# 72 directly summed columns in three bf16 addends, with the codes copied by GpSimd

## The chip, the cores and the metric

The kernel runs on one core of one Trainium2 chip. That core has a matrix engine (PE, with its weight loads shown as PEld), a vector engine (DVE), an activation engine (ACT), a general engine (POOL, also called GpSimd) and a sequencer that only issues transfers (SP). Each works through a queue of its own, in order; they meet at semaphores. The metric is the device time of the kernel in microseconds. Before the change it is 2163.95 us, the median of three runs from 2160.82 to 2169.29.

## The reference

A graph layer over 6250 nodes with 128 features. There are 206250 edges, each with a row of 128 floats and a node number `src` that stands in no order. The edge rows are summed per node, and a small network follows with a residual and a layer norm:

```python
row = edge_index[0]                                   # src, 206250 numbers in 0..6249
edge_aggr = jnp.zeros((n, 128)).at[row].add(edge_attr)
combined = concatenate([x, edge_aggr, global_feat repeated], -1) @ W_c + b_c
h = softplus(combined @ W1 + b1)
h = softplus(h @ W2 + b2)
out = layernorm(x + h @ W3 + b3)
```

Nearly all of the time goes into `edge_aggr`, the scatter-add.

## The kernel before, in words

An edge *column* is 128 edges, one on each partition; there are 1611 full ones and a rest of 42 edges. Nodes are cut into 25 *blocks* of 256. `sums_t` holds the sums of all nodes on chip, features on the partitions and nodes along the free axis.

**The sorted way.** Most columns are cut into ten groups (`GROUPS`). For a group, `positions` works out on DVE and PE at which row of a buffer in HBM (`place`) each edge has to stand, so that edges of one block lie together. POOL then issues one indirect DMA per column (`scatter_rows`, L644), which writes 128 rows of 129 floats: the 128 features and a *code*, the node's number within its block plus an offset that belongs to the group. The rows come from HBM in pieces of ten columns (`load_rows`, three pieces ahead, five buffers), and the code of each edge is copied into the row's last float by `code_rows`, on ACT, two pieces ahead (L636). When a group is in place, `reduce_steps` reads it back in chunks on SP, DVE compares the codes with a row of numbers to make a 0/1 matrix `hot` (L423), PE multiplies rows by it (L437) and DVE adds the result to the block's part of `sums_t` (L454). For the last two groups ACT makes three of four `hot` matrices (L418, L420), since DVE has more to do there. While group g is scattered, group g-1 is summed and the positions of group g+1 are made. Three `place` buffers go round, and are filled with -1 at first.

**The direct way.** The first 48 columns (`DIRECT`) are not scattered. For each column and each window of 512 nodes, ACT makes a 0/1 matrix out of |node - number| (L577, two columns) and relu(1 - that) (L579, both at once), PE multiplies the edge rows by it (L589, f32), and after 12 columns (`SET`) DVE adds the window's sum to `sums_t` (L593). A *job* is two columns (`QUAD`) by one window; PE's part of a job stands two jobs behind ACT's. `begin` prepares `less`, the node numbers less each window's first node, for all columns at once.

**The order of the work.** PE, DVE, ACT and SP run in an order written out by hand: for every piece of every group, the row load, the code copy and the scatters are emitted, then a share of the steps for positions, sums, node rows, fills and direct jobs. The shares go by `AHEAD`, and the direct steps go to groups 1 to 6 in proportion to `left`, an estimate of the column times that a group has to spare. All of SP's transfers stand in one queue, so a chunk load that waits for a buffer holds up the row loads behind it. POOL alone is ordered by the scheduler. The network at the end starts when all sums are there.

The code that tells which share goes where:

```python
left[g] = max(0.0, groups[g][1] - groups[g][0]
              - groups[g - 1][3] * groups[g - 1][2] / 3 - (9 if 3 <= g < 6 else 0))
```

Of the kernel before, what the change touches and what calls it, by code (L numbers as in the profile page):

```python
# [7 lines left out]
F32 = mybir.dt.float32  # L8
BF16 = mybir.dt.bfloat16
# [7 lines left out]
P = 128  # L17
# [2 lines left out]
LOAD_COLS = 10  # L20
EPS = 1e-5

GROUPS = ((40, 1), (120, 2), (200, 4), (240, 4), (240, 4), (240, 4), (212, 4), (140, 2), (88, 2),
          (44, 1))
CHUNK_ROWS = 1024
PLACES = 3

DIRECT = 48
SET = 12
WIDE = 512  # L30
QUAD = 2
FILL = 4
POS_COLS = 20
PART_COLS = 60
# [6 lines left out]
LEAD = 3  # L41
# [6 lines left out]
def kernel(  # L48
# [119 lines left out]
    with ExitStack() as phase:  # L168
# [376 lines left out]
        def direct_steps():  # L545


            steps = []
            if not ND:
                return steps  # L550
            NW = -(-NB * BL // WIDE)
            less = keep.tile([P, NW, ND], F32, name="less")
            rows_in, hot_of, sum_of = {}, {}, {}

            def begin():

                first = keep.tile([P, NW], F32, name="first")
                nc.gpsimd.iota(first, pattern=[[WIDE, NW]], base=0, channel_multiplier=0,
                               allow_small_or_imprecise_dtypes=True)
                part, node, _ = whole_nodes(0, ND)  # L560
                nc.vector.tensor_copy(node, part)
                nc.vector.tensor_tensor(
                    less, node.unsqueeze(1).to_broadcast([P, NW, ND]),
                    first.unsqueeze(2).to_broadcast([P, NW, ND]), op=ALU.subtract)

            def load(c):
                n = min(SET, ND - c)
                rows_in[c] = direct_p.tile([P, SET, D], F32, name="direct_rows", bufs=2)
                sync_dma(rows_in[c][:, :n],
                         edge_attr[:P * T, :].rearrange("(p t) d -> p t d", p=P)[:, c:c + n, :])  # L570

            def compare(c, w, q):
                n = min(WIDE, NB * BL - w * WIDE)
                hot = direct_p.tile([P, QUAD, WIDE], F32, name="direct_hot", bufs=4)
                hot_of[c, w, q] = hot
                for j in range(QUAD):
                    nc.scalar.activation(hot[:, j, :n], iota_f[:, :n], AF.Abs,  # L577
                                         bias=less[:, w, c + q + j:c + q + j + 1], scale=-1.0)
                nc.scalar.activation(hot[:, :, :n], hot[:, :, :n], AF.Relu, bias=ones[:, :1],  # L579
                                     scale=-1.0)  # L580

            def add(c, w, q):
                n = min(WIDE, NB * BL - w * WIDE)
                k = min(SET, ND - c)
                hot = hot_of.pop((c, w, q))
                if q == 0:
                    sum_of[c, w] = ps.tile([P, WIDE], F32, name="direct_sum", bufs=2)
                for j in range(QUAD):
                    nc.tensor.matmul(sum_of[c, w][:, :n], rows_in[c][:, q + j, :], hot[:, j, :n],  # L589
                                     start=(q + j == 0), stop=(q + j == k - 1))  # L590
                if q + QUAD == k:
                    here = sums_t[:, w * WIDE:w * WIDE + n]
                    nc.vector.tensor_add(here, here, sum_of.pop((c, w))[:, :n])  # L593

            jobs = [(c, w, q) for c in range(0, ND, SET) for w in range(NW)
                    for q in range(0, min(SET, ND - c), QUAD)]
            steps += [begin, lambda: load(0)]
            for i in range(len(jobs) + 2):
                def one(i=i):
                    if i < len(jobs):  # L600
                        c, w, q = jobs[i]
                        if (w, q) == (NW // 2, 0) and c + SET < ND:
                            load(c + SET)
                        compare(*jobs[i])
                    if i > 1:
                        add(*jobs[i - 2])
                steps.append(one)
            return steps
# [22 lines left out]

        def code_rows(i):
            if i >= len(pieces):
                return
            g, c, k, r = pieces[i]
            nc.scalar.copy(rows_at[i][:r, :k, D:W], low[:r, c:c + k].unsqueeze(2))  # L636

        def scatter_rows(i):
            g, c, k, r = pieces[i]
# [12 lines left out]
        with tc.manual_schedule(engines={ET.PE, ET.DVE, ET.Activation, ET.SP}):  # L652
# [20 lines left out]
            while put["todo"]:  # L673
                put["todo"].pop(0)()
            node_codes(ND, c1)
            for i in range(LEAD - 1):
                code_rows(i)
            for step in positions(0):
                step()
            sync_dma(wc_sb, w_c.rearrange("(k p) d -> p k d", p=P))  # L680
# [10 lines left out]
            for g in range(1, G - 3):  # L691
                left[g] = max(0.0, groups[g][1] - groups[g][0]
                              - groups[g - 1][3] * groups[g - 1][2] / 3 - (9 if 3 <= g < 6 else 0))
            direct_at = 0.0
            i = 0
            assert G > 6
            nodes = []
            for g in range(G):
# [11 lines left out]
                filled = fill_rows(g + 1)  # L710
                done = [0, 0, 0, 0]
                for q in mine:
                    load_rows(i + LEAD)
                    code_rows(i + LEAD - 1)
                    scatter_rows(i)
                    i += 1

                    now = []
                    for w, todo in enumerate((prep, sums, other, filled)):
                        share = (q - mine[0] + 1) / len(mine)  # L720
                        if w == 2:
# [175 lines left out]
```

## Time and profile before

| what | value |
|---|---|
| median of three runs | 2163.95 us |
| the profiled execution's own time | 2166.67 us |
| its span, first to last instruction | 2164.9 us |
| mean granted clock of PE | 0.925 |
| scatters on POOL (L644) | 1564, 961 ns each, first at 25.57 us, last at 2018.42 us |
| direct products on PE (L589) | 1248 instructions, 559.0 us busy |
| sorted products on PE (L437) | 4472 instructions, 1106.0 us busy |
| direct matrices on ACT (L577, L579) | 624 and 312, 404.6 and 348.0 us busy |
| code copies on ACT (L636) | 159, 30.7 us busy |

A line of the list of groups reads: line of the kernel, engine, operation, what it writes and reads, count, then the busy time and the mean of one, then the idle time of that engine just before these instructions and what ended most of it. A line of a timeline reads: start, length, engine, line, operation, count, and in brackets the idle time before it with its releaser. A line of windows gives, for a stretch of the span, its length, the busy time and count of PE, PEld, DVE, ACT and POOL, then the granted clock, the share of the DMA engines and GB/s. A line of waits gives who waited for whom, the total, how often and the longest. "issue" means that the engine waited for nothing that the profile shows. Busy times of PE contain the length of a product through its pipeline, so products that follow each other closely overlap: their pitch, from start to start, is what they cost.

The groups' scatters start at 25.6, 81.2, 233.1, 486.2, 789.9, 1102.6, 1406.2, 1675.6, 1852.7 and 1964.0 us.

### The profile page before, as it was taken

How to read it: one execution, taken by the hardware profiler on the slowest of the kernel's cores; microseconds unless marked ns; L12 is line 12 of the kernel's file. 1: busy time of each engine (PE TensorE's matmuls, PEld its weight loads, DVE VectorE, ACT ScalarE, POOL GpSimd, SP SyncE). 2: the span in 40 equal slices, each digit the busy share in tenths (PEclk: the TensorE clock that was granted, in tenths of full speed). 3: DMA queues.
4: the chain of work that ended last, by engine and by line, in shares of the span. 5: the costliest groups of instructions: out<-in, count | busy, mean ns of one | idle time of the engine just before them, and what ended most of it. 6: DMA issues, size and time to landing. Idle time of an engine off the chain costs nothing.

```text
span 2164.9 us, 22230 instructions
## 1 busy us (share of the span) xinstructions
PE 1789.7 (83%) x6415; PEld 1209.0 (56%) x6415; DVE 1328.0 (61%) x1923; ACT 912.7 (42%) x1350; POOL 1560.2 (72%) x1631
## 2 busy tenths in 40 slices
PE   3398788966889878999889998788998899688884
PEld 0144445534555555666556666556666778566752
DVE  7386457524656345675465855355755798796567
ACT  0476665653444335444353443353342000006964
POOL 5777777777777767777777777777777777777226
PEclk8699999987999999999999999999999999899997
DMA  9998788738786665676756666556766687776521
GB/s 299 303 313 270 216 256 251 231 101 262 213 225 189 194 193 148 188 207 188 198 173 180 194 190 175 169 167 189 202 198 170 211 245 227 214 213 199 151 75 60
DMA packets 415376, 435.50 MB, mean 201 GB/s; under 512 B 37743, under 2 KB 305766, under 8 KB 415254
## 3 DMA queue, kind: packets, MB, share of 16 engines
q1 hardware_dynamic: 365062, 330.71, 54.9%
q0 software_dynamic: 50048, 103.35, 14.4%
q8 instruction: 51, 0.84, 0.2%
q14 instruction: 71, 0.58, 0.1%
q10 hardware_dynamic: 144, 0.02, 0.0%
HBM read 260.90 MB, written 173.03 MB: 200 GB/s over the span
## 4 chain that ended last, share of the span: by engine, by line
PE 57%; DVE 15%; POOL 9%; issue 7%; DMA 6%; ACT 4%; DVEq 1%; SPq 0%; POOLq 0%; ACTq 0%
PE part L437 37%; PE direct_sum L589 16%; POOL place L644 8%; DVE hot L423 7%; DMA place<-rows,pos 4%; DVE sums_t L454 2%; ACT hot L418 2%; DVE so_far L316 1%; DVE sums_t L593 1%; DMA rows<-in_edge_attr 1%; DMA chunks<-place 1%; PE small L339 1%; POOL y L833 1%; DVEq L448 1%; DVE pos L350 1%
## 5 line engine op out<-in xcount | busy, mean ns | idle before, releaser
L644 POOL DMA_INDIRECT place<-rows,pos x1564 | 1503.2, 961 | 509.0 <-issue 443.5
L437 PE MATMUL part<-hot,chunks 128*128 128x256 f32 x4472 | 1106.0, 405 | 267.8 <-DVE hot L423 250.9
L437 PEld LDWEIGHTS part<-hot,chunks 128*128 128x128 f32 x4472 | 894.9, 203 | 507.8 <-DVE hot L423 310.5
L577 ACT ACTIVATE direct_hot<-iota_f,less 128x512 f32<-128x512 f32 (+1 forms) x624 | 404.6, 695 | 811.0 <-PE direct_sum L589 808.1
L423 DVE SCALAR_TENSOR_TENSOR hot<-chunks,iota_ps 128x2048 f32<-128x2048 f32 (+1 forms) x261 | 592.2, 2270 | 44.2 <-DMA chunks<-place 44.2
L589 PE MATMUL direct_sum<-direct_hot,direct_rows 128*128 128x512 f32 (+1 forms) x1248 | 559.0, 580 | 29.4 <-DMA direct_rows<-in_edge_attr 25.6
L454 DVE TENSOR_TENSOR sums_t<-sums_t,part 128x256 f32 x781 | 327.1, 419 | 133.3 <-PE part L437 110.8
L589 PEld LDWEIGHTS direct_sum<-direct_hot,direct_rows 128*128 128x128 f32 x1248 | 233.3, 190 | 232.2 <-issue 204.9
L579 ACT ACTIVATE direct_hot<-direct_hot,ones 128x1024 f32<-128x1024 f32 (+1 forms) x312 | 348.0, 1115 | 10.1
L593 DVE TENSOR_TENSOR sums_t<-sums_t,direct_sum 128x512 f32<-128x512 f32 (+1 forms) x52 | 34.7, 667 | 410.5 <-PE direct_sum L589 410.5
L636 ACT COPY rows<-src_i 128x10 f32<-128x10 f32 (+1 forms) x159 | 30.7, 196 | 360.3 <-DMA place<-rows,pos 328.9
L350 DVE TENSOR_REDUCE pos<-at 128x20 int32<-128x500 f32 (+2 forms) x80 | 87.0, 1087 | 2.7
L316 DVE TENSOR_TENSOR_SCAN so_far<-iota_ps,ib 128x1500 bf16<-128x1500 f32 (+5 forms) x29 | 85.7, 2955 | 0.0
L418 ACT ACTIVATE hot<-iota_f,chunks 128x256 f32<-128x256 f32 x156 | 64.2, 493 | 26.7 <-DMA chunks<-place 24.2
L845 POOL TENSOR_TENSOR x_sb<-x_sb,b_all 128x512 f32<-128x512 f32 (+1 forms) x13 | 15.2, 1219 | 67.8 <-DMA x_sb<-in_x 67.8
L348 DVE TENSOR_TENSOR at<-small,ib 128x500 f32<-128x500 f32 (+2 forms) x80 | 52.9, 661 | 4.2 <-PE small L339 3.5
L833 POOL TENSOR_SCALAR y<-y,mv,rs 128x128 f32<-128x128 f32 (+1 forms) x45 | 35.2, 796 | 19.9 <-DVE rs L827 19.0
L262 DVE TENSOR_TENSOR ib<-block,iota_ps 128x1500 bf16<-128x1500 bf16 (+5 forms) x29 | 44.2, 1550 | 0.0
L273 PE MATMUL small<-ib,ones_h 128*128 128x500 bf16 (+2 forms) x80 | 23.8, 406 | 23.9 <-DVE ib L262 23.9
L536 DVE TENSOR_SCALAR z_x<-small,z_bias 128x512 f32<-128x512 f32 (+1 forms) x13 | 9.3, 718 | 51.3 <-PE small L534 51.3
L335 PE MATMUL small<-so_far,ones_h 128*128 128x500 bf16 (+2 forms) x80 | 31.4, 393 | 11.1 <-DVE last L319 11.1
L420 ACT ACTIVATE hot<-hot,ones 128x2048 f32<-128x2048 f32 (+1 forms) x20 | 39.2, 1960 | 0.7
(115 smaller groups left out, 472.7 us busy)
## 6 DMA issues: line engine op xcount, KB each, us to landing
chunks<-place SPq DMA_DIRECT2D x278, 516.0 KB, 4.5
rows<-in_edge_attr SPq DMA_DIRECT2D x155, 640.0 KB, 6.7
place<-fill SPq DMA_DIRECT2D x252, 258.0 KB, 8.3
place<-rows,pos POOLq DMA_INDIRECT x1564, 4.5
x_sb<-in_x SPq DMA_DIRECT2D x24, 256.0 KB, 4.6
direct_rows<-in_edge_attr SPq DMA_DIRECT2D x4, 768.0 KB
out<-y SPq DMA_DIRECT2D x12, 256.0 KB, 2.2
chunks<-place SPq DMA_DIRECT2D x3, 258.0 KB, 3.2
```

The lines of the kernel that those rows point to most:

```text
L316: nc.vector.tensor_tensor_scan(t, iota_ps[:, 1:2].to_broadcast([P, NB * n]), in_block[k][0], 0.0, op0=ALU.mult, op1=ALU.add)
L350: nc.vector.tensor_reduce(pos[:, a - c0 + j0:a - c0 + j1], at.rearrange("p b g -> p g b"), axis=mybir.AxisListType.X, op=ALU.add)
L418: nc.scalar.activation(hot[:, j], codes, AF.Abs, bias=chunks[i][:, j, D:W], scale=-1.0)
L423: nc.vector.scalar_tensor_tensor(hot[:, :m], chunks[i][:, :m, D:W].to_broadcast([P, m, BL]), code_of(g), iota_ps.unsqueeze(1).to_broadcast ...
L437: nc.tensor.matmul(part[:, s - q, :], t[:, s * sub + j, :D], hot[:, s * sub + j], start=(j == 0), stop=(j == sub - 1))
L454: nc.vector.tensor_add(here, here, part[:, s - q, :])
L577: nc.scalar.activation(hot[:, j, :n], iota_f[:, :n], AF.Abs, bias=less[:, w, c + q + j:c + q + j + 1], scale=-1.0)
L579: nc.scalar.activation(hot[:, :, :n], hot[:, :, :n], AF.Relu, bias=ones[:, :1], scale=-1.0)
L589: nc.tensor.matmul(sum_of[c, w][:, :n], rows_in[c][:, q + j, :], hot[:, j, :n], start=(q + j == 0), stop=(q + j == k - 1))
L593: nc.vector.tensor_add(here, here, sum_of.pop((c, w))[:, :n])
L644: s = nc.gpsimd.indirect_dma_start(out=dst, out_offset=bass.IndirectOffsetOnAxis(ap=at, axis=0), in_=rows[:r, j, :], in_offset=None)
L833: engine.tensor_scalar(y[:r, q, :], y[:r, q, :], mv[:r, at + q, 0:1], rs[:r, 1, at + q:at + q + 1], op0=ALU.subtract, op1=ALU.mult)
```

## The change

- `DIRECT` is 72 instead of 48, and the seventh group (group 6, counted from 0) has 188 columns instead of 212. The other groups keep their sizes and take their columns 24 further on.
- The direct products are made in bf16. An f32 row is split into three bf16 numbers that add up to it: its upper 16 bits (read in place), the upper 16 bits of the rest, and what remains. The second is written over the lower 16 bits of the row, the third into `direct_low`. `split` does this on DVE for 12 columns at a time, two columns per instruction (`SPLIT`). PE reads the first two with a stride of two and makes three bf16 products where one f32 product stood. The 0/1 matrix is made in bf16.
- `less` is made per set of 12 columns in `split` instead of once in `begin`.
- The first direct load is issued before the last piece of group 0, ahead of that piece's row load; it was in group 1.
- `code_rows` runs on POOL in front of the piece's own scatters, instead of on ACT two pieces ahead.

```diff
-GROUPS = ((40, 1), (120, 2), (200, 4), (240, 4), (240, 4), (240, 4), (212, 4), (140, 2), (88, 2),
+GROUPS = ((40, 1), (120, 2), (200, 4), (240, 4), (240, 4), (240, 4), (188, 4), (140, 2), (88, 2),
           (44, 1))
-DIRECT = 48
+DIRECT = 72
+SPLIT = 2
...
-            less = keep.tile([P, NW, ND], F32, name="less")
+            node_f = keep.tile([P, ND], F32, name="node_f")
+            first = keep.tile([P, NW], F32, name="first")
...
-                part, node, _ = whole_nodes(0, ND)
-                nc.vector.tensor_copy(node, part)
-                nc.vector.tensor_tensor(
-                    less, node.unsqueeze(1).to_broadcast([P, NW, ND]),
-                    first.unsqueeze(2).to_broadcast([P, NW, ND]), op=ALU.subtract)
+                part, _, _ = whole_nodes(0, ND)
+                nc.vector.tensor_copy(node_f, part)
...
+            def halves(t):
+                return [t.bitcast(BF16).rearrange("p c (d h) -> p c d h", h=2)[:, :, :, h]
+                        for h in (0, 1)]
+
+            def split(c):
+                n = min(SET, ND - c)
+                less = less_of[c] = direct_p.tile([P, NW, SET], F32, name="less", bufs=2)
+                nc.vector.tensor_tensor(
+                    less[:, :, :n], node_f[:, c:c + n].unsqueeze(1).to_broadcast([P, NW, n]),
+                    first.unsqueeze(2).to_broadcast([P, NW, n]), op=ALU.subtract)
+                low_in[c] = direct_p.tile([P, SET, D], BF16, name="direct_low", bufs=2)
+                for a in range(0, min(SET, ND - c), SPLIT):
+                    b = min(a + SPLIT, SET, ND - c)
+                    rest = direct_p.tile([P, SPLIT, D], F32, name="direct_rest")[:, :b - a]
+                    x_c = rows_in[c][:, a:b]
+                    nc.vector.tensor_sub(rest, x_c, halves(x_c)[1])
+                    nc.vector.tensor_sub(low_in[c][:, a:b], rest, halves(rest)[1])
+                    nc.vector.tensor_copy(halves(x_c)[0], halves(rest)[1])
...
-                hot = direct_p.tile([P, QUAD, WIDE], F32, name="direct_hot", bufs=4)
+                hot = direct_p.tile([P, QUAD, WIDE], BF16, name="direct_hot", bufs=4)
...
-                for j in range(QUAD):
-                    nc.tensor.matmul(sum_of[c, w][:, :n], rows_in[c][:, q + j, :], hot[:, j, :n],
-                                     start=(q + j == 0), stop=(q + j == k - 1))
+                for j in range(q, q + QUAD):
+                    addends = halves(rows_in[c][:, j:j + 1]) + [low_in[c][:, j:j + 1]]
+                    for i, part in enumerate(addends):
+                        nc.tensor.matmul(sum_of[c, w][:, :n], part[:, 0], hot[:, j - q, :n],
+                                         start=(j == 0 and i == 0), stop=(j == k - 1 and i == 2))
...
-            steps += [begin, lambda: load(0)]
+            steps += [lambda: load(0), begin, lambda: split(0)]
...
+                        if (w, q) == (NW - 2, 0) and c + SET < ND:
+                            split(c + SET)
...
         def code_rows(i):
-            if i >= len(pieces):
-                return
             g, c, k, r = pieces[i]
-            nc.scalar.copy(rows_at[i][:r, :k, D:W], low[:r, c:c + k].unsqueeze(2))
+            nc.gpsimd.tensor_copy(rows_at[i][:r, :k, D:W], low[:r, c:c + k].unsqueeze(2))
...
-            for i in range(LEAD - 1):
-                code_rows(i)
...
+            direct_first = direct[:1]
+            direct = direct[1:]
...
+                    if g == 0 and q == mine[-1]:
+                        for step in direct_first:
+                            step()
                     load_rows(i + LEAD)
-                    code_rows(i + LEAD - 1)
+                    code_rows(i)
                     scatter_rows(i)
```

More of the change, by code (lines that the diff above doesn't have):

```diff
@@ L551, in direct_steps @@
             NW = -(-NB * BL // WIDE)
-            less = keep.tile([P, NW, ND], F32, name="less")
-            rows_in, hot_of, sum_of = {}, {}, {}
+            node_f = keep.tile([P, ND], F32, name="node_f")
+            first = keep.tile([P, NW], F32, name="first")
+            less_of = {}
+            rows_in, low_in, hot_of, sum_of = {}, {}, {}, {}
             def begin():
-                first = keep.tile([P, NW], F32, name="first")
                 nc.gpsimd.iota(first, pattern=[[WIDE, NW]], base=0, channel_multiplier=0,
                                allow_small_or_imprecise_dtypes=True)
-                part, node, _ = whole_nodes(0, ND)
-                nc.vector.tensor_copy(node, part)
-                nc.vector.tensor_tensor(
-                    less, node.unsqueeze(1).to_broadcast([P, NW, ND]),
-                    first.unsqueeze(2).to_broadcast([P, NW, ND]), op=ALU.subtract)
+                part, _, _ = whole_nodes(0, ND)
+                nc.vector.tensor_copy(node_f, part)
             def load(c):
@@ L577, in compare @@
                     nc.scalar.activation(hot[:, j, :n], iota_f[:, :n], AF.Abs,
-                                         bias=less[:, w, c + q + j:c + q + j + 1], scale=-1.0)
+                                         bias=less_of[c][:, w, q + j:q + j + 1], scale=-1.0)
                 nc.scalar.activation(hot[:, :, :n], hot[:, :, :n], AF.Relu, bias=ones[:, :1],
```

## The prediction

> **What bounds the kernel now.** First the page's engine totals, then POOL's waits, since no engine's share alone says which one sets the pace.
>
> ```profile
> PE 1789.7 (83%) x6415; PEld 1209.0 (56%) x6415; DVE 1328.0 (61%) x1923; ACT 912.7 (42%) x1350; POOL 1560.2 (72%) x1631
> ...
> L644 POOL DMA_INDIRECT place<-rows,pos x1564 | 1503.2, 961 | 509.0 <-issue 443.5
> L437 PE MATMUL part<-hot,chunks 128*128 128x256 f32 x4472 | 1106.0, 405 | 267.8 <-DVE hot L423 250.9
> ```
>
> PE shows the larger share, but POOL has no real idle time: 443.5 of its 509.0 us are the gap of 0.30 us in front of every scatter. The waits, POOL's alone:
>
> ```profile
> POOL place L644 <- issue: 443.5, 1456, 0.3
> ...
> POOL place L644 <- DMA w_sb<-in_L_gnn_W: 18.4, 1, 18.4
> POOL place L644 <- DMA place<-rows,pos: 16.8, 55, 0.3
> POOL place L644 <- ACT rows L636: 12.3, 7, 9.3
> POOL place L644 <- DMA rows<-in_edge_attr: 4.9, 2, 4.6
> ```
>
> The first scatter starts at 25.57 us, the last ends at 2019.33: 1564 scatters at 0.961 + 0.305 = 1.266 us are 1979 of those 1994 us. So POOL runs through, and a column of edges costs 1.266 us there. The only real stall in the middle, POOL's timeline:
>
> ```profile
> 800.01 0.96 POOL L644 DMA_INDIRECT place<-rows,pos  x1 [0.31 <-issue]
> 801.28 0.96 POOL L644 DMA_INDIRECT place<-rows,pos  x1 [0.30 <-issue]
> 811.52 0.96 POOL L644 DMA_INDIRECT place<-rows,pos  x1 [9.28 <-ACT rows L636]
> ```
>
> and ACT's at that place, where the code copy that POOL waits for stands in the queue behind direct work that waited for PE:
>
> ```profile
> 806.05 1.33 ACT L577 ACTIVATE direct_hot<-iota_f,less 128x512 f32<-128x512 f32 x2 [8.02 <-PE direct_sum L589]
> ...
> 811.05 0.19 ACT L636 COPY rows<-src_i 128x10 f32<-128x10 f32 x1
> ```
>
> The copy ends at 811.24 and the scatter starts at 811.52: 0.28 us after its release, no later than behind another scatter (0.305).
>
> Behind the scatters of group 8 (they end at about 1964) comes a fixed tail of some 200 us: the chain runs through the landing scatter, ACT's matches of group 8, then the dense layers. Last group's scatters lie beside those matches:
>
> ```profile
> 1967.82 5.06 DMA place<-rows,pos
> 1973.14 1.53 issue
> 1974.86 3.20 ACT hot L418 x8
> ```
>
> PE follows POOL closely and is second. The windows of groups 2, 4 and 6:
>
> ```profile
> 233.00:486.00 253.00, 203.06 (x636) 121.89 (x636) 132.22 (x185) 147.59 (x206) 192.21 (x200) 0.91 0.73 217
> 800.00:1104.00 304.00, 272.32 (x958) 181.55 (x956) 180.73 (x211) 134.29 (x186) 224.05 (x234) 0.95 0.66 188
> 1408.00:1677.00 269.00, 241.06 (x879) 168.00 (x878) 161.53 (x192) 107.20 (x154) 203.28 (x213) 0.96 0.64 185
> ```
>
> PE (first pair) is at 80 to 90% there. What matters is whether SP's row loads come in time, because SP is one ordered queue in which a chunk load that waits for PE holds up the row loads behind it. SP's timeline before group 7, whose first scatter is at 1675.57:
>
> ```profile
> 1655.50 5.53 SPq L145 DMA_DIRECT2D chunks<-place  x2
> 1661.32 13.41 SPq L145 DMA_DIRECT2D rows<-in_edge_attr  x4
> ```
>
> The first of the four is that group's first load: issued 14.2 us ahead, landing takes 6.7 us by the page. Elsewhere the lead, worked out in the same way, is 27 to 55 us. So there is cover, least of all at the end of group 6.
>
> **The change, part by part.**
>
> *24 columns fewer to scatter.* All come from group 6 (212 to 188), before the fixed tail: 24 x 1.266 = **-30.4 us** on POOL.
>
> *ACT no longer feeds POOL.* 159 copies (196 ns each) leave ACT. POOL's 12.3 us behind them hold 7 x 0.30 of ordinary gap: **-10.2 us**. What is late next there: the row loads, which had landed.
>
> *156 copies enter POOL.* In the built order almost every ten scatters have one copy before them, at group starts two to four together; a copy waits for no load (it writes the code's column only), and the first scatter after it waits for the copy's own semaphore. Four lie before the first scatter (under the 18.4 us wait) and four beside the tail's matches, so 148 are on the path. No POOL copy is in the trace. Nearest below: POOL's iota of 13 columns, 142 ns; the same copy on ACT, 190 to 196 ns; far above: a TENSOR_TENSOR of 128 columns, 454 ns. Ordinary POOL instructions follow each other with no gap (8 y instructions of 796 ns in 6.35 us), and a scatter released by a semaphore starts 0.28 us later instead of 0.305. So I take 0.17 for the copy, less 0.03: 0.15 us, 148 x 0.15 = **+22 us**. Low end 0.142 - 0.03 = 0.11: 16 us. High end 0.454 and one more gap of 0.305: 0.76, or 112 us. I stay at the low rows, being nearest in columns.
>
> *Direct sums in bf16, 72 columns instead of 48.* PE's timeline prices both:
>
> ```profile
> 1014.91 3.60 PE L589 MATMUL direct_sum<-direct_hot,direct_rows 128*128 128x512 f32 x8
> 1018.35 0.38 PE L334 MATMUL small<-ib,upto_h 128*128 128x500 bf16 x1
> 1018.56 0.37 PE L335 MATMUL small<-so_far,ones_h 128*128 128x500 bf16 x1
> ```
>
> An f32 product of 512 columns is two instructions at a pitch of 3.44 / 8 = 0.43; a bf16 one of 500 has a pitch of 0.21, so 0.215 for 512. Before: 1152 x 0.43 + 96 halves x 0.215 = 516 us. After: 2592 x 0.215 + 216 x 0.108 = 581. That is +65 us, less 48 instructions of L437 x 0.216 = 10. The steps are dealt out over groups 1 to 6 by the slack formula, so it comes to +12, +17, +16, +14, +14 and -9 us. It lies beside POOL's 152, 253, 304, 304, 304 and 242 us: it fits (about 90% of group 4), at the expense of the lead.
>
> *ACT:* 468 jobs instead of 312, at 2.41 us (two Abs and one Relu, 811.14 to 813.55). Group 2 gets 99 of them: 238 us in 253. ACT's output in bf16 may cost less, not more, in time; I take the same. Off the path, cover 6%.
>
> *DVE:* per pair of columns two subtractions and a strided copy of 256 elements. Nearest: node tensor_tensor of 240, 409 ns, and the cast, 285 ns: 2 x 0.43 + 0.3 = 1.2 us, 36 times = 42 us, in six lumps of 7 us; 26 more L593 sums at 688 ns, 18 us; less 3 matches of 2.28 and 6 sums of 0.42. Net about +51 on 1328 us busy. A lump holds up one DVE match, hence PE for some 5 us: cover is the lead of 27 us or more. The last split falls in group 5.
>
> *SP:* two direct loads more (768 KB), three row loads and three chunk loads fewer; the first direct load passes the last row loads of group 0 and one of them waits 2.6 us longer at the 299 GB/s of those slices, with 35 us of lead. *begin* only writes fewer elements. Nothing.
>
> *Pacing.* Group 6 loses 24 columns of time (30.4 us), gets 19 copies (2.9) and 9 us of PE work less: its closing lead falls by some 18 us, from 14.2 to below the 6.7 that landing takes. POOL then stalls 0 to 11 us. I take **+5 us**.
>
> The new subtractions read two SBUF tensors, as the node codes' additions do. Beside those (817 to 821 us) the scatters took 986 and 963 ns against 962; at that rate 108 instructions cost POOL at most 3 us. I count nothing. A rule speaks against this: the Trainium skill's GPSIMD Engine Reference, section Key points, has GpSimd share its SBUF interfaces with VectorE and contend with DVE instructions that have two SBUF inputs or run in a two-port mode. Were POOL to stand still through the whole split by that rule, the sum would be 42 us longer; the rows above show nothing of that size.
>
> **Sum:** -30.4 - 10.2 + 22 + 5 = -13.6. The profiled execution took 2166.67 (span 2164.9 and 1.8 around it), so 2153.1; it lies 2.7 above the median of 2163.95, so **2150 us**.
>
> **Rivals.**
> 1. *POOL's copy drains its pipeline (ends slower).* If the copy takes ACT's 0.196 and a gap of 0.305 opens ahead of it, as ahead of every scatter, it costs 0.47: 70 us instead of 22, and the time is 2198. It decides from (30.4 + 10.2 - 5) / 148 = 0.24 us per copy. For it: every scatter has that gap, whatever released it. Against: the gapless y instructions.
> 2. *Row loads starve POOL.* SP's waits in group 6 are 163.8 us for PE against 16.3 for POOL: PE sets its position. If the +14 to +17 us of groups 2 to 5 and the lumps are not won back at group starts, POOL stalls about 35 us instead of 5: 2180. Against: the lead recovers from 27 to 48 us within three pieces at each group start.
> 3. *The copy hides in the 0.30 gap.* Then 148 copies cost nothing and nothing stalls: -40.6, about 2124. For it: a wait released late cost no more than the gap. Against: the copy must end before its scatter is released.
> 4. *POOL stands still beside the split*, for the split's own 42 us at most: up to 2192. Against: the 986 and 963 ns above.
>
> **How the numbers follow.** Forecast 0.50 (own range 2139 to 2164: copies at 0.11 and no stall, copies at 0.22 and 8 us of stall); rivals 0.26, 0.10, 0.10, 0.04. 0.5% is 10.8 us, about what three runs spread over 8.5 us can tell. Below 2153: 0.33 of the forecast and rival 3, 0.43. Above 2175: 0.02 of the forecast, 0.22 + 0.08 + 0.04 of the others, 0.36. Between: 0.21. The range 2130 to 2200 leaves out most of rival 3 and the upper part of rival 1.
>
> **What would show it.** 1540 scatters still at 1.266; POOL copies of 0.13 to 0.22 us and the scatter after one starting within 0.3 us of its end (right), or a start-to-start over a copy above 1.55 us (rival 1). No wait of POOL for ACT. The direct products at a pitch of 0.215 us; a pitch near 0.43 would make PE the bound. POOL waits for row loads above 10 us in all: rival 2. The tail after group 8's last scatter unchanged near 200 us.

## The result: 4.5% slower

The changed kernel takes 2260.55 us, the median of four runs from 2258.58 to 2263.83, against 2163.41 us of the kernel before. The ratio is 1.045, with a 95% interval from 1.0434 to 1.0467. The profiled execution took 2258.58 us, with a span of 2256.8 us, 91.9 us more than the span before. The predicted 2150 us and the range from 2130 to 2200 us both miss it.

The engines' totals and two groups of the changed kernel's page:

```profile
PE 1837.4 (81%) x7815; PEld 1232.4 (55%) x7922; DVE 1370.1 (61%) x2051; ACT 1249.7 (55%) x1659; POOL 1568.1 (69%) x1763
...
L671 POOL DMA_INDIRECT place<-rows,pos x1540 | 1480.5, 961 | 592.8 <-issue 406.4
...
L619 DVE TENSOR_TENSOR sums_t<-sums_t,direct_sum 128x512 f32<-128x512 f32 (+1 forms) x78 | 52.0, 667 | 540.8 <-PE direct_sum L615 540.8
```

ACT is 337 us busier (55% of the span instead of 42%), by the matrices of 24 more columns; PE's busy time grows by 48 us and DVE's by 42. POOL's idle time, which before was almost only the 0.30 us ahead of each scatter, has another part now. POOL's waits (total, times, longest):

```profile
POOL place L671 <- issue: 406.4, 1327, 2.1
POOL place L671 <- DMA rows<-in_edge_attr: 111.9, 29, 8.3
...
POOL place L671 <- DMA place<-rows,pos: 16.5, 54, 0.3
POOL place L671 <- POOL rows L663: 15.6, 92, 0.8
...
POOL place L671 <- DVE sums_t L456: 11.7, 9, 7.1
```

POOL waits for row loads, 111.9 us in 29 places, where before it waited 4.9 us in two. The starts of the scatters in POOL's timeline account for the whole difference. Two scatters that follow each other directly start 1.266 us apart, before (1560 pairs) and after (1409). Over one copy it is 1.326 us (83 pairs); 15 intervals with two to four copies and one of 1.95 us raise the mean of all such intervals without a stall to 1.356 us (99). All other intervals together exceed the plain pitch by 129.3 us, against 14.5 before. So: 24 scatters fewer, -30.4; 99 intervals with copies at 0.09, +8.9; the stalls, with the copies in them, +114.8; the plain pitch, 1409 x 0.0007, +1.0; a first scatter 0.1 earlier and a tail behind the last scatter 2.4 shorter, -2.5. The sum is +91.8, and the span is 91.9 longer. The loss is POOL standing still, nearly all of it for rows, in groups 3 to 6 but for the one place near 82 us that the kernel before has too. At seven of the stalls the profile names work of DVE or a code copy as what came last (0.8 to 7.1 us); there too the rows had been asked for only 6.4 to 7.4 us earlier.

**Why the rows come late.** SP's timeline and POOL's at one of the stalls:

```profile
1049.73 13.09 SPq L147 DMA_DIRECT2D chunks<-place  x2
1063.18 0.37 SPq L147 DMA_DIRECT2D rows<-in_edge_attr  x1
```

```profile
1063.52 0.21 POOL L663 COPY rows<-src_i 128x10 f32<-128x10 f32 x1
1070.12 0.98 POOL L671 DMA_INDIRECT place<-rows,pos  x1 [6.39 <-DMA rows<-in_edge_attr]
```

Two chunk loads occupy SP's queue for 13 us, most of it waiting for a free buffer; the row load behind them goes out at 1063.18 us, and POOL, which is done with its copy at 1063.73, starts on those rows at 1070.12. The lead of a row load, from its issue to the first scatter of its rows, was 27 to 55 us almost everywhere before. After, it falls in the second half of group 3 to 8 to 17 us. In groups 4 to 6 it recovers to 34 to 41 us by the fifth or sixth piece of a group, is down to 10 to 15 us with the seventh, and then mostly 6 to 10 us, hardly more than the landing takes (6.5 us).

**Why the chunk loads come late.** A chunk buffer comes free when PE has multiplied it. DVE's timeline beside that SP stall, at the end of a split:

```profile
1046.63 0.31 DVE L583 TENSOR_TENSOR less<-node_f,first 128x156 f32<-128x156 f32 x1
1046.86 0.42 DVE L591 TENSOR_TENSOR direct_rest<-direct_rows 128x256 f32<-128x256 f32 x1
1047.31 0.42 DVE L592 TENSOR_TENSOR direct_low<-direct_rest 128x256 bf16<-128x256 f32 x1
1047.65 0.33 DVE L594 COPY direct_rows<-direct_rest 128x256 bf16<-128x256 bf16 x1
...
1053.44 0.30 DVE L594 COPY direct_rows<-direct_rest 128x256 bf16<-128x256 bf16 x1
1053.65 2.28 DVE L425 SCALAR_TENSOR_TENSOR hot<-chunks,iota_ps 128x2048 f32<-128x2048 f32 x1
1055.84 0.86 DVE L456 TENSOR_TENSOR sums_t<-sums_t,part 128x256 f32 x2
...
1063.77 0.69 DVE L619 TENSOR_TENSOR sums_t<-sums_t,direct_sum 128x512 f32<-128x512 f32 x1 [7.06 <-PE direct_sum L615]
1064.37 0.67 DVE L350 TENSOR_TENSOR at<-small,ib 128x500 f32<-128x500 f32 x1
1065.08 1.10 DVE L352 TENSOR_REDUCE pos<-at 128x20 int32<-128x500 f32 x1
1066.09 2.29 DVE L425 SCALAR_TENSOR_TENSOR hot<-chunks,iota_ps 128x2048 f32<-128x2048 f32 x1
```

and PE's:

```profile
1055.98 6.46 PE L439 MATMUL part<-hot,chunks 128*128 128x256 f32 x16 [4.03 <-DVE hot L425]
...
1068.43 5.36 PE L439 MATMUL part<-hot,chunks 128*128 128x256 f32 x16 [3.41 <-DVE hot L425]
```

Two things are to be seen. The split keeps DVE for 7.0 us (1046.63 to 1053.65), the match behind it comes late, and PE stands 4.03 us. Then DVE itself stands 7.06 us, because the direct window's sum (L619) was written out right behind PE's last product of that window and DVE works in order. Behind that sum stand steps of the positions and the next match, which needed nothing from PE; PE runs out of matrices meanwhile and stands 3.41 us. DVE waits for PE and PE for DVE, by turns.

PE is slow behind these two gaps: 16 products behind a gap of 0.46 us (at 1045.98 us) last 3.72 us at a granted clock of 1.00, these two lots 6.46 us at 0.57 and 5.36 us at 0.69. This does not tell the two kernels apart: over groups 3 to 6 the granted clock is 0.94 before and 0.95 after, and the sorted products are busy for 645.2 and 639.3 us. The Trainium skill's page TensorE: Matmul & The Clock Gate, section HAM oscillation, gives the rule that PE should have no idle gap above about 3.4 us, since it is put back to half its clock behind one. These two gaps agree with it; but a lot at 1006.80 us, behind a gap of 2.03 us only, lasted 5.41 us at a granted clock of 0.68.

### The profile page after: what moved, and what is told of

Same layout as the page of the kernel before. It is cut to its first block, busy times and chain, and to the rows that moved or that the text cites. A ratio compares the mean times of both kernels' runs of the same rounds, so it can differ in the third digit from the quotient of the medians.

```text
span 2256.8 us, 25013 instructions
## 1 busy us (share of the span) xinstructions
PE 1837.4 (81%) x7815; PEld 1232.4 (55%) x7922; DVE 1370.1 (61%) x2051; ACT 1249.7 (55%) x1659; POOL 1568.1 (69%) x1763
## 4 chain that ended last, share of the span: by engine, by line
PE 56%; DVE 19%; ACT 12%; issue 5%; DMA 4%; POOL 2%; DVEq 1%; SPq 1%; POOLq 0%; ACTq 0%
PE part L439 35%; PE direct_sum L615 17%; DVE hot L425 8%; ACT direct_hot L601 4%; ACT direct_hot L603 4%; DVE sums_t L456 3%; ACT hot L420 2%; DMA place<-fill 2%; DVE so_far L318 2%; POOL place L671 2%; DVE sums_t L619 1%; SPq L147 1%; DMA chunks<-place 1%; PE small L341 1%; DVEq L450 1%
## 5 line engine op out<-in xcount | busy, mean ns | idle before, releaser
L439 PE MATMUL part<-hot,chunks 128*128 128x256 f32 x4424 | 1088.4, 404 | 261.7 <-DVE hot L425 243.9
L601 ACT ACTIVATE direct_hot<-iota_f,less 128x512 bf16<-128x512 f32 (+1 forms) x936 | 604.3, 692 | 676.4 <-PE direct_sum L615 615.2
L425 DVE SCALAR_TENSOR_TENSOR hot<-chunks,iota_ps 128x2048 f32<-128x2048 f32 x258 | 585.2, 2269 | 3.0 <-DMA chunks<-place 2.8
L615 PE MATMUL direct_sum<-direct_hot,direct_rows 128*128 128x512 bf16 (+1 forms) x1773 | 518.8, 371 | 80.9 <-ACT direct_hot L603 47.7
L603 ACT ACTIVATE direct_hot<-direct_hot,ones 128x1024 bf16<-128x1024 bf16 (+1 forms) x468 | 521.9, 1115 | 15.2
L619 DVE TENSOR_TENSOR sums_t<-sums_t,direct_sum 128x512 f32<-128x512 f32 (+1 forms) x78 | 52.0, 667 | 540.8 <-PE direct_sum L615 540.8
L615 PE MATMUL direct_sum<-direct_hot,direct_low 128*128 128x512 bf16 (+1 forms) x928 | 344.9, 372 | 4.9
L615 PEld LDWEIGHTS <-direct_rows 128*128 128x128 bf16 x1872 | 181.2, 98 | 284.6 <-issue 79.9
L615 PEld LDWEIGHTS <-direct_low 128*128 128x128 bf16 x936 | 91.6, 98 | 103.4 <-issue 1.1
L352 DVE TENSOR_REDUCE pos<-at 128x20 int32<-128x500 f32 (+1 forms) x79 | 85.5, 1082 | 2.7
L350 DVE TENSOR_TENSOR at<-small,ib 128x500 f32<-128x500 f32 (+1 forms) x79 | 52.0, 658 | 4.4 <-PE small L341 3.8
L337 PE MATMUL small<-so_far,ones_h 128*128 128x500 bf16 (+1 forms) x79 | 31.0, 393 | 10.4 <-DVE last L321 10.4
```

What stands on the lines that cost most here:

```text
L350: nc.vector.tensor_mul(at, got.pop((k, j0)), in_block[k][1][:, :, j0:j1])
L352: nc.vector.tensor_reduce(pos[:, a - c0 + j0:a - c0 + j1], at.rearrange("p b g -> p g b"), axis=mybir.AxisListType.X, op=ALU.add)
L425: nc.vector.scalar_tensor_tensor(hot[:, :m], chunks[i][:, :m, D:W].to_broadcast([P, m, BL]), code_of(g), iota_ps.unsqueeze(1).to_broadcast ...
L439: nc.tensor.matmul(part[:, s - q, :], t[:, s * sub + j, :D], hot[:, s * sub + j], start=(j == 0), stop=(j == sub - 1))
L601: nc.scalar.activation(hot[:, j, :n], iota_f[:, :n], AF.Abs, bias=less_of[c][:, w, q + j:q + j + 1], scale=-1.0)
L615: nc.tensor.matmul(sum_of[c, w][:, :n], part[:, 0], hot[:, j - q, :n], start=(j == 0 and i == 0), stop=(j == k - 1 and i == 2))
```

## The experiments

### The direct sums taken off DVE's critical place

The changed kernel, with one thing moved: DVE adds a window's sum not right behind PE's last product of it, but when PE is half-way through the next window, three of its six jobs later. PE's, ACT's and POOL's work, the split and the number of DVE's instructions stay the same.

```diff
+LATE = 3
...
                 if q + QUAD == k:
-                    here = sums_t[:, w * WIDE:w * WIDE + n]
-                    nc.vector.tensor_add(here, here, sum_of.pop((c, w))[:, :n])
+                    late.append((c, w, n))
+            late = []
+            def add_late():
+                c, w, n = late.pop(0)
+                here = sums_t[:, w * WIDE:w * WIDE + n]
+                nc.vector.tensor_add(here, here, sum_of.pop((c, w))[:, :n])
...
                         compare(*jobs[i])
+                    if late and i > 1 and jobs[i - 2][2] == LATE * QUAD:
+                        add_late()
                     if i > 1:
                         add(*jobs[i - 2])
+                    if i == len(jobs) + 1:
+                        add_late()
```

> The changed kernel with DVE's addition of a direct window's sum moved three jobs behind the last product of that window, so that DVE, which works in order, does not stand behind PE (78 such waits are 541 us of idle DVE in the changed kernel, and the next chunk's match waits behind each). Theory DVE: PE's waits for the match (244 us) fall, the row loads come earlier, 2170 to 2220. Theory PE or ACT: PE's own work is unchanged, 2235 to 2260.

It took 2141.49 us, against 2168.95 of the kernel before on the same chip, one run each: 119 us below the changed kernel's median and 1.3% below the kernel before. The theory that DVE's place in the queue matters had asked for 2170 to 2220 us: right in direction, and the gain was larger than it said. The waits of DVE and PE (whole span):

```profile
DVE sums_t L626 <- PE direct_sum L616: 61.4, 23, 12.7
...
PE part L440 <- DVE hot L426: 155.1, 48, 37.6
```

POOL:

```profile
POOL place L682 <- issue: 404.6, 1327, 0.3
...
POOL place L682 <- POOL rows L674: 19.0, 122, 0.2
...
POOL place L682 <- DMA rows<-in_edge_attr: 10.0, 4, 9.1
```

The wait for the direct sums falls from 540.8 to 61.4 us, PE's for matches from 243.9 to 155.1, and POOL's for row loads from 111.9 to 10.0, of which 9.1 is the one place near 86 us, ahead of group 1's first scatter. What SP waits for in groups 3 to 6 shows best who sets the pace. In the kernel before (486.2 to 1675.6 us):

```profile
SPq L145 <- PE part L437: 629.4, 138, 7.1
SPq L145 <- DVE hot L423: 183.7, 46, 18.5
SPq L145 <- DMA place<-rows,pos: 130.5, 41, 11.9
```

In the changed kernel (491 to 1768 us):

```profile
SPq L147 <- PE part L439: 691.5, 147, 7.5
SPq L147 <- DVE hot L425: 302.1, 63, 29.8
SPq L147 <- PE small L528: 56.0, 6, 14.9
SPq L147 <- DMA place<-rows,pos: 29.1, 6, 12.1
```

and with the sums delayed (494.5 to 1651 us):

```profile
SPq L148 <- DMA place<-rows,pos: 815.9, 216, 12.2
SPq L148 <- PE part L440: 115.3, 44, 4.5
SPq L148 <- PE direct_sum L616: 6.4, 16, 0.9
SPq L148 <- PE small L361: 3.7, 1, 3.7
```

Before the change SP waited mostly for PE and DVE already; with 72 columns it waits for almost nothing else. With the sums delayed it waits for the scatters, that is for POOL, which then runs without a stall behind group 1's first scatter, the row loads of groups 3 to 6 leading by 45 to 50 us. Its sum: -30.4 for the scatters, 126 intervals with copies at 0.0875 = +11.0, stalls 9.6 instead of 14.5 = -4.9, first scatter +0.9, tail -2.4, plain pitch +0.4: -25.4, and the span is 25.2 shorter than before's 2164.9. So the 115 us of stalls hang on where DVE's sum stands in its queue, with 72 direct columns. That PE has too much to do, or that ACT makes its matrices too slowly, is refuted as a sufficient cause: both did the same work here, and PE waited for ACT's matrices no less (53.6 us in all against 47.7).

### Everything but the 24 columns

The changed kernel with 48 direct columns and 212 in group 6, as before: three bf16 addends, the split, and the copies on POOL remain.

```diff
-GROUPS = ((40, 1), (120, 2), (200, 4), (240, 4), (240, 4), (240, 4), (188, 4), (140, 2), (88, 2),
+GROUPS = ((40, 1), (120, 2), (200, 4), (240, 4), (240, 4), (240, 4), (212, 4), (140, 2), (88, 2),
...
-DIRECT = 72
+DIRECT = 48
```

> The changed kernel with 48 direct columns and group 6 at 212: bf16 products, split and POOL copies stay, sums not delayed. On the chips where the kernel before took over 2800 us this question could not be put. Theory DVE (DVE standing behind PE in the direct sums): 52 waits as before, each behind less PE work (389 us of direct products against 516), four splits of 7 us instead of six: no stall of POOL above 15 us, 2155 to 2175. If bf16 and the split are harmful by themselves: above 2190.

It took 2168.02 us against 2161.74, one run each: a difference of 0.3%, no more than runs of the kernel before differ among themselves (2160.82 to 2169.29). POOL's waits:

```profile
POOL place L671 <- issue: 415.9, 1364, 0.3
...
POOL place L671 <- POOL rows L663: 18.8, 121, 0.2
...
POOL place L671 <- DMA direct_rows<-in_edge_attr: 7.7, 1, 7.7
```

Behind group 1's first scatter (84 us) there is no stall for rows; the lead is 45 to 50 us in groups 3 to 6. DVE's wait for direct sums is 317.9 us, less than before's 410.5, as the direct products need less of PE (387 us by the pitches, against 516). The mean interval with copies is 1.347 us (129): 0.081 x 129 = 10.4 us for the copies, and 6.6 us of stalls less. SP's longest wait between 490 and 1680 us:

```profile
SPq L147 <- DMA place<-rows,pos: 848.3, 232, 12.4
```

So the copies, the split and the bf16 products together neither gain nor cost time that could be measured here. They do make room in the loop of PE and DVE, since SP now waits for POOL; 24 more columns use up more than that room, unless the sums are delayed. Those columns make up the loss of some 92 us (2260.55 less 2168.02, the second a single run).

### One part at a time, on chips where the question could not be put

The other kernels came to run on chips where the kernel before itself took 2813 to 2900 us instead of 2164, at a granted clock of 0.82 to 0.84. The trace shows there gaps that no event of the trace ends. The share of the chain in the kernel with only the POOL copies:

```profile
PE 39%; another core or an unknown queue 28%; DVE 15%; issue 12%; ACT 5%; DVEq 1%; DMA 0%
```

On such a chip all engines wait, so a part's cost in the undisturbed kernel can't be read off. The ratios are each to the kernel before on the same chip; the changed kernel itself was not run on such a chip.

Only the copies on POOL (kernel before; `code_rows` on POOL right ahead of the piece's scatters):

```diff
-            nc.scalar.copy(rows_at[i][:r, :k, D:W], low[:r, c:c + k].unsqueeze(2))
+            nc.gpsimd.tensor_copy(rows_at[i][:r, :k, D:W], low[:r, c:c + k].unsqueeze(2))
...
-                    code_rows(i + LEAD - 1)
+                    code_rows(i)
```

> The kernel before, with the code copies alone moved from ACT to POOL: 48 columns, f32 products. The changed kernel's trace has such a copy at 0.21 us, and start to start over it 1.32 us against 1.265 without: 0.06 us each. All theories of the changed kernel's slowness (too much PE work, DVE held up, ACT too slow) leave this alone: 159 x 0.06 = +9 us, less the 10 us that POOL waited for ACT: 2158 to 2168. If the copies on POOL were the cause after all, it would be above 2200.

2938.85 against 2824.16 us, 1.038 [1.028, 1.048]. On another such chip:

> The kernel before with the code copies alone moved from ACT to POOL. From the changed kernel's trace a copy lengthens the start-to-start time from 1.265 to 1.32 us: 155 x 0.06 = +9, less the 10 us that POOL waited for ACT: 2158 to 2168, no difference. Above 2190 the copy would have a cost that the trace does not show.

2998.53 against 2877.55 us, 1.044 [1.036, 1.051].

The changed kernel with the copies back on ACT, two pieces ahead:

```diff
-            nc.gpsimd.tensor_copy(rows_at[i][:r, :k, D:W], low[:r, c:c + k].unsqueeze(2))
+            nc.scalar.copy(rows_at[i][:r, :k, D:W], low[:r, c:c + k].unsqueeze(2))
...
-                    code_rows(i)
+                    code_rows(i + LEAD - 1)
```

> The changed kernel with the copies back on ACT, two pieces ahead. The columns alone are then to blame for everything: POOL saves the 9 us of copies but waits for ACT copies that stand behind direct work, where it now waits for row loads. 2255 to 2290, all three theories alike. Below 2200 it would be the copies.

3001.15 against 2824.16 us, 1.060 [1.050, 1.071].

48 columns in bf16, the kernel of the section above:

> The changed kernel with 48 direct columns and group 6 at 212: bf16 products, split and POOL copies stay. Theory PE (the PE instructions of groups 3 to 6 are too many): direct PE work falls from 516 us in the kernel before to 389, so POOL never starves and the time is the POOL sum, 2163 + 9 - 10 less at most 4 us of start: 2155 to 2165. Theory DVE (the splits and the sums that wait for PE hold up DVE, and PE behind it): four splits remain, so some 10 us each where they fall in groups 3 to 6, 2165 to 2185. Theory ACT (PE waits for ACT's matrices): ACT's work is that of the kernel before, 2155 to 2165.

1.056 [1.049, 1.063]. Two more times on such chips:

> The changed kernel with 48 direct columns and group 6 at 212: bf16 products, split and POOL copies stay, sums not delayed. Theory DVE: 52 waits as before, each behind less PE work (389 us of direct products against 516), four splits of 7 us instead of six: no stall of POOL above 15 us, 2155 to 2175. If bf16 and the split are harmful by themselves: above 2190.

> The changed kernel with 48 direct columns and group 6 at 212: bf16 products, split and POOL copies stay, sums not delayed; third try, the first two met chips on which the kernel before itself took over 2800 us. Theory DVE: 52 waits as before, each behind less PE work (389 us of direct products against 516), four splits of 7 us instead of six: no stall of POOL above 15 us, 2155 to 2175. If bf16 and the split are harmful by themselves: above 2190.

1.043 [1.035, 1.052] and 1.053 [1.039, 1.067]. Undisturbed, the same kernel is level with the kernel before. That is the reason for reading none of these ratios as a cost of the part.

The changed kernel without the third addend's product. Its result leaves out the part of each direct row below its second bf16 addend:

```diff
-                    addends = halves(rows_in[c][:, j:j + 1]) + [low_in[c][:, j:j + 1]]
+                    addends = halves(rows_in[c][:, j:j + 1])
...
-                                         start=(j == 0 and i == 0), stop=(j == k - 1 and i == 2))
+                                         start=(j == 0 and i == 0), stop=(j == k - 1 and i == 1))
```

> The changed kernel without the product of the third addend (left out: a part of every direct sum below bf16's second 8 bits); split, ACT and the copies stay. Takes a third of the direct PE work away, 194 us in all and 126 us in groups 3 to 6. Theory PE: more than the 94 us that are to be explained, POOL's stalls go, 2130 to 2150. Theory DVE or ACT: those waits remain, 2220 to 2260.

1.067 [1.054, 1.079]. Three more times, on other chips:

> The changed kernel without the product of the third addend (left out: a part of every direct sum below bf16's second 8 bits); split, ACT and the copies stay. The first try of this was on a chip where the kernel before itself took 2824 us with unexplained gaps of up to 64 us, and says nothing of the question. Takes a third of the direct PE work away, 194 us in all and 126 us in groups 3 to 6. Theory PE: more than the 94 us that are to be explained, POOL's stalls go, 2130 to 2150. Theory DVE or ACT: those waits remain, 2220 to 2260.

> The changed kernel without the product of the third addend (left out: a part of every direct sum below bf16's second 8 bits), its sums not delayed; third try, the first two met chips on which the kernel before itself took over 2800 us. Delaying the sums has brought POOL's stalls from 130 us to 9 with all of PE's work in place, so PE's amount alone is not the bound. If what counts is the time that DVE stands behind PE, a third less direct work shortens each of those waits: 2150 to 2200. If the number of such waits counts (78), 2220 or more.

> The changed kernel without the product of the third addend (left out: a part of every direct sum below bf16's second 8 bits), its sums not delayed. A third of the direct PE work goes, 126 us in groups 3 to 6; DVE's 78 sums stand where they stood. If the length of PE's work in front of each sum counts: 2150 to 2200. If the number of waits counts, whatever stands before them: 2220 or more.

1.067 [1.058, 1.076], 1.060 [1.053, 1.068] and 1.063 [1.053, 1.072]. A third of the direct work on PE was gone (some 190 us), and the kernel was still 6 to 7% slower than the kernel before there. How much of its loss the third product was can't be said, since the changed kernel has no run there, and what leaving it out does on an undisturbed chip was not seen.

The delay of the direct sums alone, in the kernel before (the same edit as above):

> The kernel before with the same three jobs' delay of DVE's direct sums; columns, f32 products and ACT copies unchanged. Theory DVE (DVE standing behind PE in the direct sums paces groups 3 to 6): POOL was hardly held up there before (9.3 and 1.5 us), so at most these 11 us come back: 2150 to 2165. Theory that the delay is a gain of its own, whatever the columns: near the 28 us or more that it gives against the kernel before in the changed one, below 2145.

0.978 [0.971, 0.986], 2806.32 against 2877.55 us. Again, on three other such chips:

> The kernel before with the same three jobs' delay of DVE's direct sums; columns, f32 products and ACT copies unchanged. Theory DVE: POOL was hardly held up there (9.3 and 1.5 us), so at most these 11 us come back: 2148 to 2165. Theory that the delay is a gain of its own, whatever the columns: below 2145.

> The kernel before with the same three jobs' delay of DVE's direct sums; columns, f32 products and ACT copies unchanged. Theory DVE: POOL was hardly held up there (9.3 and 1.5 us), so at most these 11 us come back: 2148 to 2165. Theory that the delay is a gain of its own, whatever the columns: below 2145.

> The kernel before with the same three jobs' delay of DVE's direct sums; columns, f32 products and ACT copies unchanged. Theory DVE: POOL was hardly held up there (9.3 and 1.5 us), so at most these 11 us come back: 2148 to 2165. Theory that the delay is a gain of its own, whatever the columns: below 2145.

0.976 [0.966, 0.985], one run of 2792.77 against one of 2845.38 us, and 0.981 [0.976, 0.986]: some 2% faster on all four. That is more than the 11 us (0.5%) that the theory of DVE standing behind PE had allowed, so on these chips the delay is a gain of its own.

The changed kernel with the delay, which undisturbed was 1.3% faster than the kernel before, twice on such a chip:

> The changed kernel with DVE's addition of a direct window's sum moved three jobs back, now with an interval. One look gave 2141 against 2169 for the kernel before, with no stall of POOL behind its first 60 us. Theory DVE: 2135 to 2148, ratio 0.985 to 0.992 to the kernel before. The other theories (PE's amount, ACT) leave it near 2255.

> The changed kernel with DVE's addition of a direct window's sum moved three jobs back. One look gave 2141 against 2169 for the kernel before, with no stall of POOL behind its first 61 us. Theory DVE: 2135 to 2148, ratio 0.985 to 0.992 to the kernel before. The other theories (PE's amount, ACT) leave it near 2255.

Here it was slower: 1.060 [1.052, 1.067] and 1.064 [1.055, 1.074]. POOL's longest wait in the first of these traces:

```profile
POOL place L682 <- DMA rows<-in_edge_attr: 582.7, 53, 36.3
```

with ACT's and DVE's longest waits ended by nothing in the trace. All kernels with the copies on POOL lost 4 to 7% on these chips, and the ones with the copies on ACT and 48 columns did not; but the kernel with 72 columns and the copies on ACT lost 6% too. What does that was not found.

## Why the prediction was wrong, point by point

- **Scatters.** 1540 at a pitch of 1.266 us, -30.4 us: right to the tenth.
- **ACT's waits gone.** POOL has no wait for ACT: right. "What is late next there: the row loads, which had landed" was where it went wrong: they no longer had.
- **The copies.** 0.21 to 0.22 us each, starting as the scatter ends, as here:

```profile
604.38 0.95 POOL L671 DMA_INDIRECT place<-rows,pos  x1 [0.30 <-issue]
605.33 0.22 POOL L663 COPY rows<-src_i 128x10 f32<-128x10 f32 x1
605.70 0.98 POOL L671 DMA_INDIRECT place<-rows,pos  x1 [0.16 <-POOL rows L663]
```

  The gap ahead of the scatter shrinks from 0.30 to 0.16 us, so a copy alone costs 0.06 us (1.326 less 1.266), not 0.15, and less than the low end of 0.11. At group starts two to four lie in one interval and cost 0.09 to 0.10 us each. In all they cost 9 to 11 us instead of 22. Rival 1 (0.47) falls, rival 3 (nothing) was nearer.
- **Direct products on PE.** The pitch is 0.215 us (two read with a stride of two, one plain, no difference):

```profile
1023.98 0.59 PE L615 MATMUL direct_sum<-direct_hot,direct_rows 128*128 128x512 bf16 x2
1024.42 0.38 PE L615 MATMUL direct_sum<-direct_hot,direct_low 128*128 128x512 bf16 x1
1024.63 0.59 PE L615 MATMUL direct_sum<-direct_hot,direct_rows 128*128 128x512 bf16 x2
```

  The price per product was right. The share of groups 3 to 6 was not: the trace has 1848 weight loads for them there against 796, at these pitches 382 us against 332, so 50 us more where the prediction's shares add up to 35 (the trace lacks 78 of the 1848 products, so their own records count too few).
- **"It lies beside POOL's 152, 253, 304, 304, 304 and 242 us: it fits (about 90% of group 4), at the expense of the lead."** This is the step that failed. PE's instructions fit, though less easily than said: PE was busy in 272.3 of group 4's 304 us before, so 14 us more make 94%, not 90. But PE does not run by itself: it waits for DVE's matches, 155 us in groups 3 to 6 before, and those waits are part of what a group takes. The loop of DVE and PE was full before the change already, and the prediction itself had the row: in group 6 SP waited 163.8 us for PE against 16.3 for POOL. Those four groups took 1189 us before and 1277 after. PE's record, counted from start to start within these limits, divides the 87.5 us: direct products take 54 us more, PE stands still 41 us longer (27 of them for ACT's matrices, 28 times and up to 1.5 us, and 9 for matches), and the sorted products and the rest take 8 less. So the added direct products were not laid beside the waits but came on top of them, and the waits grew too. How the 87.5 divide between the splits, the sums' place and ACT was not separated; the delay of the sums alone takes away all stalls behind group 1's first scatter.
- **The lead as cover.** "Cover is the lead of 27 us or more", used for each lump by itself, counted the same cover several times. The four groups together were 87.5 us too long, and the lead was down to 8 to 17 us within the first of them. It did recover at group starts, as the argument against rival 2 had it, but to 34 to 41 us for two or three pieces only, and the rest of each group ran without it. The +5 us for "pacing" took the last group alone.
- **Split.** 7.0 us a lump, as worked out, six of them.
- **ACT** at 2.41 us a job, as priced; "off the path, cover 6%" was too bold, since PE now waits for it 26.6 us in groups 3 to 6. That alone does not make the loss: with the sums delayed such waits are there too.
- **Rival 2**, rows starving POOL, was the mechanism, at the threshold named ("POOL waits for row loads above 10 us"). Its price of 35 us was too small: POOL's waits for rows alone grew by 107 us (111.9 less 4.9), all stalls by 115. It had been given a chance of 0.10.
- **Rival 4**, POOL standing still beside the split: in the 16 splits of three kernels the scatters beside one were longer by 0.3 to 0.7 us in all, of 7. That makes some 2.5 us in the six splits of the changed kernel, within the 3 us that the prediction had as the most.
- **The tail**: 198.7 us from group 9's first scatter, against 200.9 before. Right.

## What to carry to other kernels

Two engines that hand work to each other in fixed order are one resource: to ask whether more work fits beside a third engine, add the waits of one for the other to its busy time, not its instructions alone, and look at what the common queue (here SP's) waits for. A lead is a stock that covers a delay once; for work spread over several stages, compare the deficit per stage, times the stages, with the lead. Before giving up extra work for lack of room, look for an instruction that an in-order engine meets right when its operand is being made; here a later place for 78 sums of 0.7 us turned a loss of 4.5% into a gain of about 1.3% (the gain by one run of each kernel).

## What the runs showed of the hardware

- A small POOL copy between two indirect DMAs costs 0.06 us although it lasts 0.21 (0.09 to 0.10 each where two to four stand in a row): most of it lies in the 0.30 us that stand ahead of each indirect DMA anyway.
- Scatters beside the split do slow down, some of them to 1.16 to 1.21 us from 0.96, but by no more than 0.3 to 0.7 us in all per split of 7 us. The Trainium skill's GPSIMD Engine Reference, section Key points, has GpSimd contend with DVE instructions that have two SBUF inputs; the direction agrees, and the size here is at most a tenth of the time.
- PE's products with 128 columns of every second bf16 number as the weights have the same pitch as packed ones, 0.215 us, and their weight loads the same length, 98 ns.
- The same program took 2161 to 2169 us on some chips and 2813 to 2900 us on others, and a change's sign differed between them: the changed kernel with delayed sums is 1.3% faster than the kernel before on the one kind and 6% slower on the other. What makes the difference does not show in the trace.
- Open: the 1.3% rests on one run against one, without an interval (the account of POOL's starts gives the same 25 us); whether the delay alone helps the kernel before on an undisturbed chip was not run, though there POOL has only 14.5 us of stalls to give back. On the other chips the changed kernel itself was not run, so what the delay does to it there is open.
